# Moving row sums, projections and scaled results in a graph-attention and nucleus-diffusion kernel, and measuring the second pair's first points on VectorE

## The chip, the cores and the metric

The kernel runs on one core of a Trainium2 chip. The core has TensorE (PE, with its weight loads shown apart as PEld), VectorE (DVE), ScalarE (ACT), GpSimd (POOL) and SyncE (SP, which here only issues DMAs). Each engine works through its own queue in order; engines wait for each other by semaphores. The metric is the device time of one execution in microseconds, median over runs.

## What is computed

Two graph layers on N = 2708 nodes with 512 features, each with a layer norm and relu ahead of it and a residual around it. Layer 0 is graph attention with 8 heads of 64. Layer 1 runs two diffusion steps; each takes softmax rows of a learned similarity, keeps of every row the largest entries up to 0.9 of its mass, and mixes three products:

```
# layer 0
feats = einsum('nf,hfd->hnd', h, W)
attn  = softmax(leaky_relu(e_self + e_neigh) + mask)
x     = x + relu(einsum('hnm,hmd->hnd', attn, feats) + b)
# layer 1, steps s = 0, 1; S = adj + I
Rf = S / rowsum(S);  Rb = S / colsum(S)
A  = nucleus(softmax((Xa @ W1) @ W2 @ (Xa @ W3).T), 0.9)
Xf, Xb, Xa = Rf @ Xf, Rb @ Xb, A @ Xa
Z += Xf @ U1[s] + Xb @ U2[s] + Xa @ U3[s]
x  = x + layernorm(h + Z)
```

## The kernel before

Nodes are handled in NT = 22 tiles of 128 rows, the last with 20. "Step 1" below is the first diffusion step, s = 0 in the code; "step 2" is s = 1.

**Layer 0** works on chunks of six tiles of columns (`tchunks`: 6, 6, 6, 4), and in each chunk on two groups of four heads (`gi` = 0, 1). For each group a loop runs over all 22 row tiles `t`: VectorE makes four tiles `e` (L474), and TensorE multiplies them into PSUM banks `po` (L480). When a group is done ScalarE copies the banks out to `o_t` (L487), which frees them for the next group. At the start of a chunk the adjacency tiles are loaded (`a_f`, L449), cast on ScalarE (`a_c`, L451) and stored to `s_d` (L456). Then, for each of the chunk's tiles, `row_sums` (L337 to 349) loads the adjacency row in two halves into one buffer `arow` (SP, L345), adds each up on ScalarE (L346) and combines them on GpSimd.

What remains to be done to a tile of a finished chunk is cut into stages by `finished` (L359): `turned` transposes `o_t` into two PSUM banks (L372), `shared` divides by the sums (L388 to L397), `normed` and `cleared` make the next layer's input `v` (L416 is its relu on ScalarE), and `asked` transposes `v` (L423), copies it to `v_t` (L425), splits it into high and low parts and calls `project` (L171): eight matmul instructions (L176), two ScalarE copies (L181, L182), three GpSimd operations and a store of keys and queries. The dictionary `later` hangs these stages on steps `gi * NT + t` of the next chunk's loop (L483, L496): tile i of the old chunk has its stages at steps 3i to 3i + 3 and 3i + 5. The two banks (`pn0`, `pn1`) have one buffer each; `asked` transposes into the first and projects into the second. In the last chunk the stages run after the loop. In layer 0 the order on each engine is found by a planner, which takes what it considers ready and falls back on program order.

**Step 1 and step 2** have an order written by hand for TensorE, ScalarE, VectorE and SP (`manual_schedule`, L1293). They work on pairs of tiles (11 pairs), in a loop over g = -1 ... 10 (L1346). Pass g does the search of pair g + 1 and the attention of pair g:

- `Logits.products` (L558) multiplies queries with all keys (L567) and copies the results to `p` (L569). `p` has four buffers, so that those of pair g + 2 are those of pair g.
- `maxima` (L594, VectorE) take the row maximum; `exp` (L571) returns a list of steps: for each tile `root` and `full` (L601 with exp at half scale, L608), then `points` (GpSimd, L613 to L621), which guesses three thresholds. With `looks` there follow an empty step, twelve *looks* (ScalarE passes over `p`, L601 with `nth`: three thresholds, two functions, two tiles), and `masses` (GpSimd, L624 to L626), which makes of them the mass above each threshold.
- `search` (L734) finds the cut on VectorE. With an `Opened` handed to it, it starts from the masses of the looks (`ready`, L688; `bracket`). Without one it first measures them itself, six passes of L680 on VectorE, one for each threshold and tile. Then follow rounds of two L680, and `finish` (L874 to L809).
- In its second round `search` calls `early`, which appends the steps of the pair after next to the list `fills` and takes that pair's maxima. Before `finish` it calls `late`, in which the attention of pair g runs.
- `attended` (L1132) is a generator of twelve groups n = 0 ... 11: transpose a piece of `keep` (L1143), copy it to `at` (L1147), multiply with the values (L1165). From group `first` on it issues two steps of `fills` per group up to n = 8, then one; each group also takes one step of `others`, the products with the adjacency matrix (`part`, L1011).
- `mixed` (L1195) applies the third weight matrix (L1212), copies the results `yo` (L1219) and issues eight more fills. `late` then issues whatever fills are left.

`part` works through the adjacency products: 22 steps of loads and matmuls (L1042), then `across`, `through` (L1059) and `scaled` (L1069), which copies four results out of PSUM with a row factor and leaves their splitting (L197, L198) in the list `pending`. In pass g = -1 of step 1 there is no attention yet; `late` (L1395) issues there, in this order: four fills (root and full of both tiles of pair 1), the last `scaled`, eleven steps of the next `part`, and eleven more fills. The remaining four go into `looks` and are issued between the first groups of pair 0's attention (L1378). `pending` is emptied on VectorE after the first search (L1439).

Of the kernel before, what the change touches and what calls it, by code (L numbers as in the profile page):

```python
# [54 lines left out]
def kernel(  # L55
# [26 lines left out]
    NT = -(-N // P)  # L82
# [9 lines left out]
    G = 2  # L92
# [126 lines left out]
    with ExitStack() as l0:  # L219
# [139 lines left out]
        def finished(t, o_t, c0, bank, final):  # L359


            pr = rows[t]
            pns, held = [], []

            def turned():
                xt = work.tile([P, D], F32, name="xt0", bufs=4)
                nc.sync.dma_start(out=xt[:pr], in_=x[cols[t], :])
                held.append(xt)
                for g in range(NG):
                    pns.append(bank(g))  # L370
                    for k in range(len(beside)):
                        nc.tensor.transpose(pns[g][:pr, k * P:(k + 1) * P], o_t[:, g, k, c0:c0 + pr], ident)  # L372

            def shared():
                den = small.tile([P, H], F32, name="den")
                rden = small.tile([P, H], F32, name="rden")
                o = work.tile([P, D], F32, name="o", bufs=4)
                held.append(o)
                o3 = o.rearrange("p (h d) -> p h d", h=H)

                def halves(x, n):
                    return x[:, :2 * n].rearrange("p (i d) -> p i d", i=2)

                def turns(g):
                    return pns[g][:pr, :3 * P].rearrange("p (i d) -> p i d", i=2)

                for g in range(NG):
                    nc.vector.tensor_scalar(halves(den[:pr, g * HG:], 2), turns(g)[:, :, P::P // HG],  # L388
                                            lone_n[:pr, t:t + 1], None, op0=OP.add)
                nc.vector.reciprocal(rden[:pr], den[:pr])  # L390
                for g in range(NG):
                    c = slice(g * HG * DH, (g + 1) * HG * DH)
                    nc.vector.scalar_tensor_tensor(halves(o[:pr, c], 2 * DH), halves(fsum[:pr, c], 2 * DH),
                                                   lone[:pr, t:t + 1], turns(g)[:, :, :P], op0=OP.mult, op1=OP.add)
                eng = nc.vector if final else nc.gpsimd
                eng.tensor_mul(o3[:pr], o3[:pr], rden[:pr].unsqueeze(2).to_broadcast([pr, H, DH]))
                eng.tensor_add(o[:pr], o[:pr], b_b[:pr])  # L397

            def normed():
                xt, o = held  # L400
                nc.vector.scalar_tensor_tensor(o[:pr], o[:pr], 0.0, xt[:pr], op0=OP.max, op1=OP.add)
                held.extend(moments(small, o[:pr], pr))
                with_beta(o)

            def with_beta(o):
                xt = held[0]
                nc.gpsimd.tensor_add(xt[:pr], o[:pr], beta_b[:pr])
                nc.gpsimd.dma_start(out=xb_d[cols[t], :], in_=xt[:pr])

            def cleared():  # L410
                _, o, mean, rs = held
                v = turn.tile([P, D], F32, name="v")
                held.append(v)
                shift = small.tile([P, 1], F32, name="shift")
                nc.vector.scalar_tensor_tensor(shift[:pr], mean, -1.0, rs, op0=OP.mult, op1=OP.mult)
                nc.scalar.activation(v[:pr], o[:pr], AF.Relu, scale=rs, bias=shift[:pr])  # L416
                nc.gpsimd.dma_start(out=va_d[cols[t], :], in_=v[:pr])

            def asked():
                v = held[4]  # L420
                pt = bank(0).rearrange("p (k d) -> p k d", k=KD)
                for k in range(KD):
                    nc.tensor.transpose(pt[:, k, :pr], v[:pr, k * P:(k + 1) * P], ident[:pr, :pr])  # L423
                v_t = work.tile([P, KD, P], F32, name="v_t", bufs=2)
                nc.scalar.copy(v_t[:, :, :pr], pt[:, :, :pr])  # L425
                split_rows(halves, nc.gpsimd, v[:pr], t, vhl_d)
                project(halves, bank(1), v_t, t, 0, bufs=2)

            def rest():
                unasked.append((t, held[4]))  # L430

            return [turned, shared, normed, cleared, rest if final else asked]

        later = {}
        unasked = []
        for ci, tiles in enumerate(tchunks):
# [4 lines left out]
            for t in range(NT):  # L441
# [12 lines left out]
                    d = slice(t * P - n0, t * P - n0 + pr)  # L454
                    nc.gpsimd.tensor_tensor(a_f[:pr, d], a_f[:pr, d], ident[:pr, :pr], op=OP.add)
                nc.sync.dma_start(out=s_d[t * P:(t + 1) * P, n0:n0 + wide], in_=a_f[:, :wide])  # L456
            for t in tiles:
                row_sums(t)
            r_bs += [shares(grp, n0, cw) for grp in hgroups[1:]]
            o_t = work.tile([P, NG, len(beside), WC], F32, name="o_t", bufs=1)  # L460
            halfs = -(-cw // 512)
# [517 lines left out]
    for s in range(STEPS):  # L979
        last = s == STEPS - 1  # L980
        with ExitStack() as st:
# [136 lines left out]
            def paced(steps, n):  # L1118
                for step in steps[:n]:
                    step()  # L1120
                del steps[:n]
# [171 lines left out]
            with tc.manual_schedule(engines={PE, ACT, DVE, SP}):  # L1293
# [48 lines left out]
                    paced(loads, len(loads))  # L1342
                done = []
                ready = None
                looks, left = [], []
                for g in range(-1, NP):  # L1346

                    fills = []
# [25 lines left out]
                        fills += heads + [lambda: paced(counts, len(counts))]  # L1374
                    if g >= 0:
                        final = g == NP - 1 and not last
                        att = attended(pairs[g], *ready, fills, others, 1 if final else 3 if g else len(tgroups) + (1 if last else -1))
                    while looks:  # L1378
                        next(att)
                        paced(looks, 2)  # L1380

                    def early(g=g):
                        if g + 2 < NP:
                            fills.extend(lg[g + 2].exp())
                        first, *more = lg[g + 2].maxima if g + 2 < NP else [lambda: None]

                        def begin():
                            if g >= 0:
                                paced(pending, len(pending))
                            first()  # L1390

                        return (begin, lambda: [x() for x in more], lambda: [stats() for stats, _ in norms],
                                lambda: [rest() for _, rest in norms])

                    def late(g=g):  # L1395
# [24 lines left out]
                        if last:  # L1420
                            paced(fills, len(fills))
                        else:
                            paced(fills, 2 * G)
                            paced(others, 1)
                            others.extend(part(half, 2))
                            paced(others, NT // 2)
                            paced(fills, 2 + 3 * G * NA // 2)
                            looks.extend(fills)
                        if last:
                            paced(others, len(others))  # L1430

                    if g + 1 < NP:
                        opened = None
                        if g >= 0:
                            opened = Opened(lg[g + 1], True, junk)
                            opened.bracket()
                        ready = search(lg[g + 1], opened, junk, early, late)
# [44 lines left out]
```

## Time and profile before

Three runs took 3465.6, 3473.28 and 3474.12 us; the median is 3473.28. The profile comes from one execution more, which took 3485.01 us, with a span of 3483.2 us from the first to the last instruction. Busy time by stage, in us (a busy TensorE is not one at its peak):

| stage | from to | long | PE | DVE | ACT | POOL | granted clock |
|---|---|---|---|---|---|---|---|
| layer 0, features | 0 to 137 | 137 | 116.5 | 54.6 | 34.8 | 52.0 | 1.00 |
| layer 0, chunks | 137 to 945 | 808 | 734.6 | 716.1 | 186.3 | 295.6 | 0.94 |
| step 1 | 945 to 2185 | 1240 | 1163.7 | 684.4 | 678.8 | 285.0 | 0.98 |
| step 2 | 2185 to 3483 | 1298 | 1190.6 | 1127.6 | 601.5 | 291.0 | 0.97 |

A row of a timeline reads: start in us, length in us, engine, line of the kernel, operation, what it writes <- what it reads, shape, how many in a run, and in brackets how long the engine stood idle before and what released it. The granted clock is the share of full TensorE speed that the chip allowed in that stretch.

### The profile page before, as it was taken

To read this page: it belongs to the slowest core of one execution; us is meant where nothing else is said; L and a number is where in the kernel's file an instruction comes from. 1 tells how busy PE (TensorE), PEld (TensorE's weight loads), DVE (VectorE), ACT (ScalarE), POOL (GpSimd) and SP (SyncE) were. 2 spreads that over 40 slices of the span, in tenths; PEclk is the share of its full clock that TensorE was granted. 3 is DMA by queue.
4 is the path that set the end of the run, shared out by engine and by line. 5 is a ranking of instruction groups with operands and counts; after the bars stand their busy time and mean duration, and the time that the engine had idled before them with its cause. 6 is when DMAs were issued, how large, how long until landed. Compare 5 with 4: busy or idle time off the path is not lost. (4 is left out here: it accounts for less than half of the span.)

```text
span 3483.2 us, 44354 instructions
## 1 busy us (share of the span) xinstructions
PE 3205.4 (92%) x16033; PEld 1707.6 (49%) x16033; DVE 2582.7 (74%) x4485; ACT 1501.5 (43%) x2219; POOL 923.6 (27%) x1091
## 2 busy tenths in 40 slices
PE   8988899899988999999999999899989999988898
PEld 4542333333455446455464643555555555555554
DVE  4577899888947655463655643887999899988984
ACT  2333231011036675564667521265644554455610
POOL 4212743605231221221222222110230232213211
PEclk9998999999999999999999998999999999999999
DMA  4478554222286336244452634766444554556453
GB/s 134 157 235 267 193 169 144 75 94 80 76 299 235 113 106 208 99 166 165 142 198 98 212 112 134 263 237 203 146 156 157 202 177 144 190 175 225 150 209 123
DMA packets 240046, 580.65 MB, mean 167 GB/s; under 512 B 32863, under 2 KB 66107, under 8 KB 239657
## 3 DMA queue, kind: packets, MB, share of 16 engines
q1 hardware_dynamic: 217721, 503.38, 43.3%
q0 software_dynamic: 22064, 74.09, 5.6%
q8 instruction: 127, 2.08, 0.2%
q14 instruction: 134, 1.10, 0.1%
HBM read 471.68 MB, written 105.68 MB: 166 GB/s over the span
## 5 line engine op out<-in xcount | busy, mean ns | idle before, releaser
L1165 PE MATMUL a<-va,at 128*128 128x512 f32 (+2 forms) x1936 | 887.8, 598 | 4.9 <-ACT at L1147 4.9
L480 PE MATMUL po<-e,fw 128*32 128x384 f32 (+3 forms) x7392 | 685.1, 507 | 58.5 <-DVE e L474 29.4
L474 DVE SCALAR_TENSOR_TENSOR e<-r_b,kk,a_c 128x768 f32<-128x768 f32 (+3 forms) x704 | 667.3, 1007 | 76.9 <-PE po L480 67.9
L601 ACT ACTIVATE junk_a<-p,nth 128x2708 uint8<-128x2708 f32 (+1 forms) x240 | 612.8, 2553 | 35.3 <-POOL nth L616 30.8
L1039 PE MATMUL q<-hl,s_r 128*128 128x512 f32 x1936 | 545.4, 430 | 66.4 <-DMA s_r<-s_d 46.0
L1165 PEld LDWEIGHTS a<-va,at 128*128 128x128 f32 (+2 forms) x1936 | 338.2, 186 | 374.6 <-issue 342.8
L1039 PEld LDWEIGHTS q<-hl,s_r 128*128 128x128 f32 x1936 | 370.1, 195 | 229.4 <-issue 68.2
L480 PEld LDWEIGHTS po<-e,fw 128*32 128x32 f32 (+1 forms) x7392 | 256.0, 112 | 451.5 <-issue 270.2
L1147 ACT COPY at<-t 128x512 f32<-128x512 f32 (+3 forms) x308 | 140.8, 478 | 647.1 <-PE t L1143 643.3
L680 DVE SCALAR_TENSOR_TENSOR junk<-p,th 128x2708 bf16<-128x2708 f32 (+1 forms) x132 | 409.5, 3102 | 3.0
L1059 PE MATMUL q<-u_k,v 128*128 128x512 f32 x704 | 318.2, 594 | 1.1 <-ACT v L1049 1.1
L1042 PE MATMUL q<-s_r,hl 128*128 128x512 f32 (+1 forms) x1056 | 283.2, 414 | 28.8 <-DMA s_r<-s_d 17.9
L1042 PEld LDWEIGHTS q<-s_r,hl 128*128 128x128 f32 x1056 | 196.8, 192 | 108.5 <-issue 54.1
L1059 PEld LDWEIGHTS q<-u_k,v 128*128 128x128 f32 x704 | 134.0, 191 | 159.8 <-issue 155.0
L569 ACT COPY p<-t 128x452 f32<-128x452 f32 (+2 forms) x264 | 130.9, 537 | 172.5 <-PE t L567 131.9
L876 DVE MAX8 vn<-keep 128x8 f32<-128x2708 f32 (+1 forms) x66 | 196.8, 2981 | 2.3
L567 PE MATMUL t<-keys,q_t 128*128 128x452 f32 x528 | 156.4, 420 | 40.1 <-ACT p L569 39.5
L594 DVE TENSOR_REDUCE nmx<-p 128x1 f32<-128x2708 f32 (+1 forms) x44 | 130.5, 2967 | 65.4 <-ACT p L569 65.4
L1212 PE MATMUL a<-u_k,v_t 128*128 128x512 f32 (+1 forms) x352 | 169.0, 619 | 5.5 <-ACT yo L1219 3.3
L155 POOL TENSOR_SCALAR ln_rs<-ln_mv 128x1 f32<-128x1 f32 x66 | 49.7, 754 | 407.9 <-DVE ln_mv L154 406.7
L1143 PEld LDWEIGHTS t<-ident,keep 128*128 128x128 f32 (+1 forms) x968 | 114.7, 139 | 77.0 <-issue 47.3
L1143 PE MATMUL t<-ident,keep 128*128 128x128 f32 (+1 forms) x968 | 145.2, 272 | 3.1 <-ACT p L569 3.0
(311 smaller groups left out, 3436.2 us busy)
## 6 DMA issues: line engine op xcount, KB each, us to landing
hl<-vhl_d SPq DMA_DIRECT2D x132, 512.0 KB
s_r<-s_d SPq DMA_DIRECT2D x264, 256.0 KB
hl<-fhl_d SPq DMA_DIRECT2D x132, 512.0 KB
hl<-bhl_d SPq DMA_DIRECT2D x132, 512.0 KB
u_k<-in_L_gnn_U_dram SPq DMA_DIRECT2D x184, 256.0 KB
arow<-in_adj_dram SPq DMA_DIRECT2D x42, 677.0 KB
s_d<-a_f SPq DMA_DIRECT2D x66, 384.0 KB
s_r<-s_d SPq DMA_DIRECT2D x132, 192.0 KB
```

Source lines behind the costliest of these rows:

```text
L474: nc.vector.scalar_tensor_tensor(es[i][:pr, :cw], r_b[:pr, i, :cw], kk[:pr, t, grp[i]:grp[i] + 1], a_c[t][:pr, :cw], op0=OP.max, op1=OP.mult)
L480: nc.tensor.matmul(po[k][n][q * w:(q + 1) * w, :b - a], lhsT=of if d < DH else of.to_broadcast([pr, w]), rhs=es[i][:pr, a:b], start=(t == ...
L567: nc.tensor.matmul(pl[:, :c1 - c0], lhsT=q[:, i], rhs=self.keys[:, c0:c1], start=(i == 0), stop=(i == 1))
L601: nc.scalar.activation(junk[:pr], self.p[i][:pr], func, **kw)
L680: nc.vector.scalar_tensor_tensor(self.junk_b[:pr], p, th, p, op0=OP.is_ge, op1=OP.mult, accum_out=dst)
L876: v.max(vs, keep[0][:pr])
L1039: nc.tensor.matmul(half[j], lhsT=s_r[:, j * P:(j + 1) * P], rhs=hl[:, h], start=(c == 0 and h == 0), stop=(c == NT - 1 and h == 1))
L1042: nc.tensor.matmul(half[j][:, :w], lhsT=hl[:, h, j * P:(j + 1) * P], rhs=s_r[:, :w], start=(c == 0 and h == 0), stop=(c == NT - 1 and h == 1))
L1059: nc.tensor.matmul(half[j], lhsT=across_t[-1][k][:, j * P:(j + 1) * P], rhs=u_k, start=(start and k == 0), stop=(start and k == KD - 1))
L1143: nc.tensor.transpose(pt[:rows[c], j, :pr], keep[i][:pr, cols[c]], ident[:pr, :pr])
L1165: nc.tensor.matmul(pa[:pr], lhsT=at[:rows[c], j, :pr], rhs=va[:rows[c], c, :], start=(c == 0), stop=(c == NT - 1))
L1212: nc.tensor.matmul(pz[i][:rows[t]], lhsT=v_t[i][:, k, :rows[t]], rhs=u_k, start=(k == 0), stop=(k == KD - 1))
```

## The change

In layer 0, `asked` no longer calls `project`; a new stage `answered` does, which `later` places at step 3i + 6. `row_sums` of a chunk's tile i is no longer called ahead of the chunk's loops, but hung on step NT + 3i, in the loop of the second head group.

In step 1, pair 1 gets no looks (`exp(looks=last or g >= 0)`), and its search gets no `Opened`, so that VectorE measures its three thresholds. The list `looks` and its loop go; the fills in the attention of pair 0 begin with group 7 (`len(tgroups) + 1`) instead of group 5. In pass g = -1, the last `scaled` is issued after two fills instead of four, and `points` is the last fill. Step 2 keeps its order.

```diff
--- before.py
+++ after.py
@@ -423,13 +423,16 @@
                     nc.tensor.transpose(pt[:, k, :pr], v[:pr, k * P:(k + 1) * P], ident[:pr, :pr])
                 v_t = work.tile([P, KD, P], F32, name="v_t", bufs=2)
                 nc.scalar.copy(v_t[:, :, :pr], pt[:, :, :pr])
+                held.append(v_t)
                 split_rows(halves, nc.gpsimd, v[:pr], t, vhl_d)
-                project(halves, bank(1), v_t, t, 0, bufs=2)
+
+            def answered():
+                project(halves, bank(1), held[5], t, 0, bufs=2)
 
             def rest():
                 unasked.append((t, held[4]))
 
-            return [turned, shared, normed, cleared, rest if final else asked]
+            return [turned, shared, normed, cleared] + ([rest] if final else [asked, answered])
 
         later = {}
         unasked = []
@@ -454,8 +457,8 @@
                     d = slice(t * P - n0, t * P - n0 + pr)
                     nc.gpsimd.tensor_tensor(a_f[:pr, d], a_f[:pr, d], ident[:pr, :pr], op=OP.add)
                 nc.sync.dma_start(out=s_d[t * P:(t + 1) * P, n0:n0 + wide], in_=a_f[:, :wide])
-            for t in tiles:
-                row_sums(t)
+            for i, t in enumerate(tiles):
+                later.setdefault(NT + 3 * i, []).append(lambda t=t: row_sums(t))
             r_bs += [shares(grp, n0, cw) for grp in hgroups[1:]]
             o_t = work.tile([P, NG, len(beside), WC], F32, name="o_t", bufs=1)
             halfs = -(-cw // 512)
@@ -1342,7 +1345,7 @@
                     paced(loads, len(loads))
                 done = []
                 ready = None
-                looks, left = [], []
+                left = []
                 for g in range(-1, NP):
 
                     fills = []
@@ -1374,14 +1377,11 @@
                         fills += heads + [lambda: paced(counts, len(counts))]
                     if g >= 0:
                         final = g == NP - 1 and not last
-                        att = attended(pairs[g], *ready, fills, others, 1 if final else 3 if g else len(tgroups) + (1 if last else -1))
-                    while looks:
-                        next(att)
-                        paced(looks, 2)
+                        att = attended(pairs[g], *ready, fills, others, 1 if final else len(tgroups) + 1 if not g else 3)
 
                     def early(g=g):
                         if g + 2 < NP:
-                            fills.extend(lg[g + 2].exp())
+                            fills.extend(lg[g + 2].exp(looks=last or g >= 0))
                         first, *more = lg[g + 2].maxima if g + 2 < NP else [lambda: None]
 
                         def begin():
@@ -1420,18 +1420,18 @@
                         if last:
                             paced(fills, len(fills))
                         else:
-                            paced(fills, 2 * G)
+                            paced(fills, G)
                             paced(others, 1)
+                            paced(fills, G)
                             others.extend(part(half, 2))
                             paced(others, NT // 2)
-                            paced(fills, 2 + 3 * G * NA // 2)
-                            looks.extend(fills)
+                            paced(fills, len(fills))
                         if last:
                             paced(others, len(others))
 
                     if g + 1 < NP:
                         opened = None
-                        if g >= 0:
+                        if g >= (0 if last else 1):
                             opened = Opened(lg[g + 1], True, junk)
                             opened.bracket()
                         ready = search(lg[g + 1], opened, junk, early, late)
```

## The prediction

> **What bounds the kernel.** I read the windows by stage first, then the groups with their waits, then the timelines of single engines where TensorE stands idle. TensorE is busy 92% of 3483.2 us, so only its idle stretches can be won, or lengthened. The change touches two: the attention chunks of layer 0 (137 to 945 us, TensorE busy 734.6 of 808) and the opening of step 1 (945 to about 1205 us).
>
> Layer 0 alternates between TensorE and VectorE, which hand each other the `e` tiles. It stops dead twice, near 230 and 330 us. The 5 us windows around the first (PE, PEld, DVE, ACT, POOL busy, then granted clock, DMA share, GB/s):
>
> ```profile
> 225.00:230.00 5.00, 1.90 (x24) 0.50 (x16) 3.81 (x4) 1.43 (x2) 0.00 (x0) 0.82 0.38 109
> 230.00:235.00 5.00, 0.00 (x0) 0.00 (x0) 0.00 (x0) 1.42 (x2) 0.62 (x3) 0.50 0.40 132
> 235.00:240.00 5.00, 0.00 (x0) 0.00 (x0) 0.00 (x0) 1.73 (x4) 0.00 (x0) 0.50 0.84 316
> ```
>
> ScalarE's timeline says why: it stands in its queue at row sums whose loads are late, and the PSUM evacuations (L487) that TensorE needs come behind them.
>
> ```profile
> 232.33 1.33 ACT L346 ACTIVATE arow<-arow 128x1354 f32<-128x1354 f32 x1 [4.04 <-DMA arow<-in_adj_dram]
> 238.27 1.33 ACT L346 ACTIVATE arow<-arow 128x1354 f32<-128x1354 f32 x1 [4.52 <-DMA arow<-in_adj_dram]
> 239.60 1.98 ACT L487 COPY o_t<-po 128x384 f32<-128x384 f32 x5
> ```
>
> The second idle kind recurs once per tile in chunks 1 and 2: the projection (L176) waits for `v_t`, whose copy stands on ScalarE behind the next tile's L416. TensorE, ScalarE and VectorE timelines of one tile:
>
> ```profile
> 624.89 2.08 PE L176 MATMUL pn<-v_t,kw 128*128 128x128 f32 x8 [3.03 <-ACT v_t L425]
> ...
> 623.55 0.81 ACT L416 ACTIVATE v<-o,shift,ln_rs 128x512 f32<-128x512 f32 x1 [17.78 <-DVE shift L415]
> 624.27 0.56 ACT L425 COPY v_t<-pn 128x512 f32<-128x512 f32 x1
> ...
> 629.75 2.25 DVE L474 SCALAR_TENSOR_TENSOR e<-r_b,kk,a_c 128x768 f32<-128x768 f32 x2 [3.12 <-PE po L480]
> ```
>
> In the opening of step 1 TensorE waits for the scaled results to leave PSUM, then, at the end of pair 0, for ScalarE to be through with its looks:
>
> ```profile
> 1068.33 3.91 PE L1042 MATMUL q<-s_r,hl 128*128 128x512 f32 x10 [8.59 <-ACT yo L1069]
> ...
> 1067.61 2.40 ACT L1069 ACTIVATE yo<-q,cinv 128x512 f32<-128x512 f32 x4
> ...
> 1194.88 0.98 ACT L569 COPY p<-t 128x452 f32<-128x452 f32 x2
> ...
> 1195.48 1.12 PE L567 MATMUL t<-keys,q_t 128*128 128x452 f32 x4 [2.36 <-ACT p L569]
> ```
>
> **Row sums: counted at 0.** Layer 0 has no hand-written order; the planner places instructions by readiness, with program order as the tie-break. The loads show how far it pulls work without predecessors forward:
>
> ```profile
> L345 SPq DMA_DIRECT2D arow<-in_adj_dram x44: 302/328/807, 182.5 to 474.7; - x44
> ```
>
> Chunks 2 and 3 only begin near 572 and 780 us, yet all their row sums are loaded by 475. Moving `row_sums` down half a chunk (some 90 us) leaves it just as ready, on engines just as free (SP and ScalarE have nothing else between 200 and 240). Of all pairs that run together, the move reverses only a row sum of chunk 0 against chunk 0's first L487. So I expect the same nine ahead of L487, one load per 5.7 us, and the same stalls. Bounds: the two boundaries cost VectorE 16.0 and 18.2 us, so at best about -30 us; an unlucky new order costs up to +10.
>
> **Projection one step later: -13 us.** Nothing is added; eight L176 instructions per tile move behind the rest of the next step (38 more L480 instructions, 3.4 to 5.4 us in the timeline). `v_t` was 3.0 us late in the six worst cases, so it is there in time. TensorE waited 6.4 us at L176 in chunk 1 and 12.1 in chunk 2; VectorE idled in consequence 6.35 us (3.11, 0.52, 1.92, 0.80) and 9.9 us (3.12, 0.82, 0.90, 2.51, 2.54). What comes next is VectorE, busy otherwise, so the ceiling is its 16.2 us; chunk 3 is VectorE-bound already and gives nothing. What the move adds: the transposes of the tile after next (L372) take the bank that the projection has just filled, and so wait for L181 and L182. In chunk 2 these start 0.03 us after a typical projection and end 0.5 us later, covered by the transposes into the other bank. In chunk 1 the remaining row sums stand on ScalarE; there I keep 4 of 6.35, and 9 of 9.9 in chunk 2.
>
> A rule to weigh: the Trainium skill ("TensorE: Matmul & The Clock Gate", What's actually happening) says that the array falls to half clock only after an idle window of about 3.4 us. By it, a 3.0 us wait costs 3.0 us. The rows disagree: after it the eight projections took 2.08 us at 624.89 and 2.07 at 665.03, against 1.16 elsewhere. By the rows the six long waits are worth some 4 us more on TensorE; VectorE's ceiling takes that away again, so -13 stands either way.
>
> **Scaled results between the two root/full pairs: -8.2 us at first.** ScalarE ends the first tile's full at 57.8 (times of this part are us after 1000) and waits till 62.1 for the second maximum. The four L1069 (2.4 us) fit in there; the last product ends at 59.7, so L1042 starts there instead of at 68.33. The 11 steps after it are paced by loads that are issued as slots come free, so the whole block, 99.5 at its end, moves to about 91. The next thing due is the end of the search of pair 0 (VectorE, 91.8), which frees `p` for the L569 copies: these start at 91.9 instead of 100.08. Attention of pair 0 shifts by -8.2.
>
> **No looks for pair 1: +15.5 us.** ScalarE loses 12 looks (2.55 + 0.19 each). VectorE gains six masses; the same six for pair 0 took 1016.87 to 1035.45, 18.6 us. They stand behind the eight split pieces that end at 114.8 and wait for stores (6.91, 3.70, 1.97 us) while TensorE's loads hold the DMA queues. With the loads over by then I take 109 (the four pieces at 1237 waited only 3.19 us). Then:
>
> ```profile
> 1118.57 0.17 DVE L688 TENSOR_TENSOR pts<-top,pts 128x6 f32<-128x6 f32 x1 [3.73 <-POOL pts L626]
> ...
> 1132.29 2.97 DVE L594 TENSOR_REDUCE nmx<-p 128x1 f32<-128x2708 f32 x1
> ...
> 1142.20 2.97 DVE L594 TENSOR_REDUCE nmx<-p 128x1 f32<-128x2708 f32 x1
> ```
>
> L688 moves from 118.6 to 127.7, the maxima of pair 2 (L594) end at 144.4 and 154.3. The start of the fills moves from group 5 to 7, where the copy of `at` 8 now falls at 139.5. Root and full wait there for the first maximum (done 149.9; stall about 0.3), then for the second (done 159.8); `at` 10 comes at 160.4 where TensorE wants it at 156.6: 3.8. With the look behind it, the second `v_t` of the pair is copied by 170.2 instead of 173.8, so 3.6 of the 8.2 us remain. If the split pieces don't end sooner, 5 us more go; if they end at 106, about 3 fewer.
>
> Then the tail. Group 5 to 7 is four fills fewer in attention. In the old run five looks run there, four and three inside `mixed`, none after. In the new one it is one, four and four, with three left, which `late` issues ahead of the next pair's L569. ScalarE reaches L569 at 170.2 + 10.5 + 1.7 + 10.7 + 1.0 + 8.0 = 202.2, against 194.9: +7.3. TensorE, which waited 2.36 there, now waits about 13. The search of pair 2 begins with the same delay, so nothing later catches up: pairs 1 to 10 are TensorE-bound and merely shift.
>
> Another rule speaks against this edit: "SBUF — State Buffer" (SBUF: two separate sides) says ScalarE has ports of its own, while a VectorE operation with two SBUF inputs shuts out a GpSimd operation that reads SBUF for its whole length. The row: L618 took 4.21 us beside the masses of pair 0, 1.35 without. By the rule the 18.6 us would cost GpSimd one mass, 3 us; by the timeline it then has only stores to issue, and I count 0.
>
> **The sum.** -13 + 7.3 = -5.7 us on the profiled 3485.0 (span 3483.2 and 1.8 around it), or 3479.3. The median shown is 11.7 below the profiled time; the same difference from it gives 3468.
>
> **Rivals.** *Row sums really leave the first halves*: they spread over the second halves, L487 finds ScalarE free, both stops go (-30): about 3438. For it speaks only the wording of the edit; against it, loads at 475 us. *A new wait on the projection's bank* (slower): in chunk 1, L372 follows L176 at once, L181 and L182 stand behind a row sum whose load takes some 4.5 us, four tiles in turn: +18, chunk 1's gain lost, so -9 + 18 + 7.3 = +16, 3490. It decides from 2.7 us per tile. For it: ScalarE waits 165.8 us for these loads in all; against: old L181s there waited at most 1.3 us. *The planner puts the projections where they were*, so layer 0 gives nothing: +7, 3481.
>
> **Chances.** Forecast 0.55 (own range 3458 to 3482: layer 0 from -18 to -4, step 1 from +3 to +13), row sums 0.14, bank 0.16, no effect in layer 0 0.15. Outside 3440 to 3489 lie half of the row-sum and half of the bank case. Faster by over 0.3% (about what a measurement can tell from no change): 0.14 + 0.13 = 0.27; slower: 0.16, half of the last case: 0.24; between: 0.49.
>
> **What would show it.** Right: L346 before 240 us as now, no 3 us waits at L176, L1042 near 1060, six L680 behind the split pieces, about 13 us before L567 near 1202. Wrong: L346 only in second halves; L372 waiting for L182; no gap before L567, which would make step 1 a gain.

## The result and the profile after

The changed kernel takes 3478.42 us (median of 20 runs, 3463.52 to 3510.39), the kernel before 3473.51 us beside it. The ratio is 1.0008 with a 95% interval of 0.9991 to 1.0024: no difference that can be measured. 3468 had been forecast, with a range of 3458 to 3482, and "within 0.3%" held the largest chance. The range and the class came true; the small gain of 5.7 us does not show (by the ratio +2.8 us, -3 to +8).

Below the surface much moved. The profiled execution took 3465.86 us, some 13 below the median of its kernel, where the profile of before is some 11 above its own. So sums are read stage by stage here, over the profiles of all runs, and not from one pair. From the end of `asked` on, line numbers are 3 higher than before (L480 is now L483, L567 is L570, L1165 is L1168).

**Layer 0, the first stop.** Windows of 5 us around it, columns as in the prediction:

```profile
227.00:232.00 5.00, 0.00 (x0) 0.00 (x0) 1.54 (x2) 1.42 (x2) 0.62 (x3) 0.50 0.37 110
232.00:237.00 5.00, 0.65 (x6) 0.21 (x10) 0.00 (x0) 2.50 (x6) 0.00 (x0) 0.50 0.93 359
```

ScalarE's timeline there:

```profile
234.50 1.33 ACT L346 ACTIVATE arow<-arow 128x1354 f32<-128x1354 f32 x1 [4.39 <-DMA arow<-in_adj_dram]
...
235.84 1.98 ACT L490 COPY o_t<-po 128x384 f32<-128x384 f32 x5
```

and the loads of the tile `arow` (operation and count, then shortest, median and longest issue in ns, then first and last start):

```profile
L345 SPq DMA_DIRECT2D arow<-in_adj_dram x44: 301/328/1067, 180.7 to 469.6; - x44
```

A row sum still stands ahead of the copies of `o_t`, and the 44 loads still begin at 181 us and are through at 470. The edit moved nothing.

**Layer 0, the projection.** TensorE's timeline in chunks 1 and 2:

```profile
440.88 0.55 PE L372 MATMUL pn<-ident,o_t 128*128 128x128 f32 x3 [3.25 <-ACT kq_b L182]
...
614.25 1.16 PE L176 MATMUL pn<-v_t,kw 128*128 128x128 f32 x8 [0.46 <-ACT v_t L425]
```

The 3 us waits ahead of L176 are gone: 0.5 us is left of 18.5 in the whole layer. The feared new wait, L372 behind L182, is there once, for 3.3 us. Another new wait is not on TensorE at all: VectorE now waits for GpSimd (see e1_projection). Layer 0 ends (last L483) at 919.2 us, not at 943.5.

**Step 1.** TensorE first, then ScalarE and VectorE:

```profile
1032.14 2.41 PE L1045 MATMUL q<-s_r,hl 128*128 128x512 f32 x8
...
1066.59 7.51 PE L570 MATMUL t<-keys,q_t 128*128 128x452 f32 x20 [6.25 <-ACT p L572]
...
1135.86 6.62 PE L1168 MATMUL a<-va,at 128*128 128x512 f32 x8 [3.61 <-ACT at L1150]
...
1180.38 7.97 PE L570 MATMUL t<-keys,q_t 128*128 128x452 f32 x20 [11.63 <-ACT p L572]
```

```profile
1066.00 0.97 ACT L572 COPY p<-t 128x452 f32<-128x452 f32 x2 [24.82 <-DVEq L961]
...
1119.86 0.20 ACT L607 ACTIVATE nmx<-nmx 128x1 f32<-128x1 f32 x1 [5.10 <-DVE nmx L597]
...
1129.78 0.20 ACT L607 ACTIVATE nmx<-nmx 128x1 f32<-128x1 f32 x1 [3.34 <-DVE nmx L597]
...
1179.81 0.95 ACT L572 COPY p<-t 128x452 f32<-128x452 f32 x2
```

```profile
1084.50 3.03 DVE L683 SCALAR_TENSOR_TENSOR junk<-p,th_a 128x2708 bf16<-128x2708 f32 x1
...
1116.86 2.97 DVE L597 TENSOR_REDUCE nmx<-p 128x1 f32<-128x2708 f32 x1
```

L1045 no longer waits for the scaled results (8.59 us before), and the copies to `p` start in the very moment in which the search of pair 0 ends (1066.00). That is the gain. Then the six passes of VectorE begin at 1084.5, behind the split pieces, and push the maxima of pair 2 back; ScalarE waits for both, TensorE once for ScalarE (3.61 us), and at the end three looks are left over, behind which TensorE waits 11.63 us, against 2.36 before.

Lengths that can be told apart over all profiles (worked out from the starts and ends of the named instructions):

| stretch | kernels without the edit | kernels with it |
|---|---|---|
| layer 0, start to TensorE's restart after its second stop near 340 | 340.0 to 343.6, mean 341.5 (5 profiles) | 337.5 to 346.6, mean 341.5 (5, later projection) |
| from there to the first L388 of chunk 1's tiles | 230.1 to 231.9, mean 231.0 | 225.5 to 226.9, mean 226.2 |
| from there to the first L388 of chunk 2's tiles | 223.5 to 226.9, mean 226.1 | 213.1 to 213.5, mean 213.3 |
| from there to the last `po` matmul | 141.8 to 142.0 | 141.5 to 141.7 |
| step 1: end of pair 0's search (start of L969) to the L569 ahead of pair 1's attention | 100.3 to 103.1, mean 101.2 (8) | scaled results alone (e3, e5): 102.3, 101.3; no looks alone (e4): 118.7; both: 113.8, 113.8 |
| step 1, whole: to the first matmul of step 2 | 1232.4 to 1242.4, mean 1237.4 (8) | scaled results alone: 1230.6, 1239.4; no looks alone: 1257.4; both: 1246.8, 1249.7 |

So by the traces layer 0 gives 4.8 + 12.8 + 0.3 = 17.9 us. The opening of step 1 loses 113.8 - 101.2 = 12.6; over the whole of step 1 it is 1248.2 - 1237.4 = 10.8, where the kernels without the edit alone differ by 10.

### The profile page after: what moved, and what is told of

Its sections match the earlier page's. It is cut to its first block, busy times and chain, and to the rows that moved or that the text cites. A ratio compares the mean times of both kernels' runs of the same rounds, so it can differ in the third digit from the quotient of the medians.

```text
span 3464.1 us, 44348 instructions
## 1 busy us (share of the span) xinstructions
PE 3187.4 (92%) x16033; PEld 1698.3 (49%) x16033; DVE 2588.8 (75%) x4497; ACT 1471.4 (42%) x2195; POOL 928.7 (27%) x1088
## 3 DMA queue, kind: packets, MB, share of 16 engines
q8 instruction: 127, 2.08, 0.3%
## 5 line engine op out<-in xcount | busy, mean ns | idle before, releaser
L1168 PE MATMUL a<-va,at 128*128 128x512 f32 (+2 forms) x1936 | 890.5, 600 | 7.6 <-ACT at L1150 7.5
L483 PE MATMUL po<-e,fw 128*32 128x384 f32 (+3 forms) x7392 | 677.0, 503 | 61.6 <-DVE e L477 37.4
L477 DVE SCALAR_TENSOR_TENSOR e<-r_b,kk,a_c 128x768 f32<-128x768 f32 (+3 forms) x704 | 659.5, 996 | 46.7 <-PE po L483 38.1
L604 ACT ACTIVATE junk_a<-p,nth 128x2708 uint8<-128x2708 f32 (+1 forms) x228 | 582.1, 2553 | 36.4 <-POOL nth L619 32.1
L1042 PE MATMUL q<-hl,s_r 128*128 128x512 f32 x1936 | 536.3, 424 | 61.8 <-DMA s_r<-s_d 45.3
L1168 PEld LDWEIGHTS a<-va,at 128*128 128x128 f32 (+2 forms) x1936 | 339.5, 187 | 379.2 <-issue 343.7
L483 PEld LDWEIGHTS po<-e,fw 128*32 128x32 f32 (+1 forms) x7392 | 257.3, 112 | 446.3 <-issue 262.6
L1042 PEld LDWEIGHTS q<-hl,s_r 128*128 128x128 f32 x1936 | 363.1, 192 | 224.3 <-issue 68.8
L1045 PE MATMUL q<-s_r,hl 128*128 128x512 f32 (+1 forms) x1056 | 279.9, 409 | 16.7 <-DMA s_r<-s_d 15.1
L1045 PEld LDWEIGHTS q<-s_r,hl 128*128 128x128 f32 x1056 | 193.2, 189 | 95.7 <-issue 53.4
L572 ACT COPY p<-t 128x452 f32<-128x452 f32 (+2 forms) x264 | 132.4, 536 | 197.1 <-PE t L570 116.5
L570 PE MATMUL t<-keys,q_t 128*128 128x452 f32 x528 | 162.5, 433 | 58.0 <-ACT p L572 57.4
```

The source lines that it names most:

```text
L477: nc.vector.scalar_tensor_tensor(es[i][:pr, :cw], r_b[:pr, i, :cw], kk[:pr, t, grp[i]:grp[i] + 1], a_c[t][:pr, :cw], op0=OP.max, op1=OP.mult)
L483: nc.tensor.matmul(po[k][n][q * w:(q + 1) * w, :b - a], lhsT=of if d < DH else of.to_broadcast([pr, w]), rhs=es[i][:pr, a:b], start=(t == ...
L570: nc.tensor.matmul(pl[:, :c1 - c0], lhsT=q[:, i], rhs=self.keys[:, c0:c1], start=(i == 0), stop=(i == 1))
L604: nc.scalar.activation(junk[:pr], self.p[i][:pr], func, **kw)
L1042: nc.tensor.matmul(half[j], lhsT=s_r[:, j * P:(j + 1) * P], rhs=hl[:, h], start=(c == 0 and h == 0), stop=(c == NT - 1 and h == 1))
L1045: nc.tensor.matmul(half[j][:, :w], lhsT=hl[:, h, j * P:(j + 1) * P], rhs=s_r[:, :w], start=(c == 0 and h == 0), stop=(c == NT - 1 and h == 1))
```

## The experiments

| label | what runs | median, us (runs) | before beside it, us | ratio, 95% interval |
|---|---|---|---|---|
| e0_before_again | before, a second profile | 3472.01 (1) | 3474.98 | |
| e1_projection | later projection alone | 3462.95 (22) | 3474.98 | 0.9972, 0.9959 to 0.9984 |
| e2_row_sums | row sums' edit alone | 3476.57 (20) | 3478.69 | 0.9992, 0.9980 to 1.0004 |
| e3_scaled | scaled results alone | 3477.59 (14) | 3474.98 | 1.0010, 0.9994 to 1.0026 |
| e4_no_looks | no looks alone | 3491.63 (12) | 3474.98 | 1.0046, 1.0031 to 1.0061 |
| e5_proj_scaled | projection and scaled results | 3467.44 (22) | 3478.09 | 0.9968, 0.9956 to 0.9981 |
| e7_first5 | changed kernel, fills from group 5 | 3467.39 (6) | 3478.69 | 0.9973, 0.9942 to 1.0004 |
| e8_after_again | changed kernel again | 3478.18 (14) | 3478.09 | 1.0002, 0.9982 to 1.0022 |
| e12_held_alone | row sums held back by `e` | 3521.79 (4) | 3478.69 | 1.0114, 1.0097 to 1.0131 |
| e9_held | the same, later projection | 3515.74 (4) | 3478.69 | 1.0086, 1.0063 to 1.0109 |
| e13_second_half | row sums held back by `o_t` | 3460.22 (21) | 3473.69 | 0.9959, 0.9948 to 0.9970 |
| e14_second_half_proj | the same, later projection | 3448.26 (6) | 3473.69 | 0.9931, 0.9909 to 0.9953 |

### The parts one at a time

**e0_before_again** has no edit.

> The kernel before once more, to see what one execution differs from another by. Layer 0's last L480 came at 943.0 us in its first profile and at 918.7 in that of the changed kernel; step 1, from there to the first matmul of step 2, took 1242.9 us against 1247.3. Theory (these are properties of the kernels): 943 within 4 us and 1243 within 3. Rival (the spread of 10 us and more between runs of one kernel lies in layer 0's loads): layer 0 ends elsewhere, by 8 us or more, and the 24 us between the two profiles are partly luck.

It took 3472.01 us; layer 0 ended at 937.2 and step 1 took 1239.9 us, against 943.5 and 1242.4 in the first profile. Layer 0 is 6.3 us off, beyond the 4 us of the theory and short of the 8 of the rival. This is the scatter against which the rest is read.

**e1_projection**

```diff
+                held.append(v_t)
...
-                project(halves, bank(1), v_t, t, 0, bufs=2)
+            def answered():
+                project(halves, bank(1), held[5], t, 0, bufs=2)
...
-            return [turned, shared, normed, cleared, rest if final else asked]
+            return [turned, shared, normed, cleared] + ([rest] if final else [asked, answered])
```

> The projection's step alone moves. Theory: no wait of 3 us at L176 is left, layer 0 ends 10 to 17 us earlier than in the kernel before, step 1 is as long as before; ratio 0.995 to 0.998. Rival (layer 0's gain comes from the row sums): L176's waits go, but layer 0 ends within 4 us of before, since VectorE or the wait of L372 for L182 takes the place; ratio 0.999 to 1.001.

By the medians it is worth 3475 x 0.0028 = 9.7 us (5.6 to 14.2). In the trace layer 0 ends at 920.2; L372 waits once, 4.0 us, for L182. So the gain is real, and the rival with the bank is an event of a single tile. What VectorE waited for in chunk 2 (us in total, times, longest), in the kernel before:

```profile
DVE e L474 <- PE po L480: 20.4, 12, 4.2
```

and in this one:

```profile
DVE o L401 <- POOL o L397: 9.3, 4, 2.4
DVE e L477 <- PE po L483: 3.0, 3, 2.5
```

The wait for TensorE falls by 17.4 us, and a wait for GpSimd that was not there before takes 9.3 of them. It stands behind L397: when a tile's L396 and L397 fall due, GpSimd is still at the projection of an earlier tile (L186 to L189), and from L390 to the end of L397 it takes 5.0 and 5.7 us in two tiles, against 3.9 before. In chunk 1 the same two waits go from 12.2 to 4.1 and from 2.6 to 11.3 us, which cancel out.

**e2_row_sums**

```diff
-            for t in tiles:
-                row_sums(t)
+            for i, t in enumerate(tiles):
+                later.setdefault(NT + 3 * i, []).append(lambda t=t: row_sums(t))
```

> Only the edit that moves the row sums. Theory: the planner undoes it, the program is the old one with other buffer numbers, so the ratio is 1.000 within its interval, the row-sum loads still run from about 182 to 475 us, and TensorE stops near 230 and 330 us as before. Rival (row sums leave the first halves): about 30 us less, ratio 0.991.

In its trace every engine runs the same instructions in the same order as in e0_before_again. Its loads of row sums run from 183.4 to 472.2 us, TensorE stops for 12.3 and 14.1 us, and the ratio is 0.9992. The planner undoes the edit, as forecast.

**e3_scaled**

```diff
-                            paced(fills, 2 * G)
+                            paced(fills, G)
                             paced(others, 1)
+                            paced(fills, G)
```

> Only the last scaled results move between the two root/full pairs; the looks stay. Theory: L1042 starts right after L1059 instead of 8.6 us later, L567 of pair 2 then waits a little for the end of the search (under 2 us), and 7 to 8 us stay to the end, since the looks end earlier too: ratio 0.997 to 0.999. Rival (nine looks between L1042 and L567 hold ScalarE): L567's copies stand behind the looks, which do not start earlier than before, so that under 2 us remain; ratio 0.9995 to 1.0005.

Nothing was gained that the medians show; it is the rival's case. TensorE's and ScalarE's timelines of this kernel:

```profile
1053.15 2.39 PE L1042 MATMUL q<-s_r,hl 128*128 128x512 f32 x8
...
1090.15 7.52 PE L567 MATMUL t<-keys,q_t 128*128 128x452 f32 x20 [9.30 <-ACT p L569]
```

```profile
1089.49 0.19 ACT L601 ACTIVATION_READ_ACCUMULATOR junk_a<-p,nth 128x1 f32 x1
1089.59 0.95 ACT L569 COPY p<-t 128x452 f32<-128x452 f32 x2
```

The wait ahead of L1042 is gone, and 37 us later the same length of wait stands ahead of L567. The search of pair 0 is over at 1083.1, but ScalarE works until 1089.5 through nine looks of pair 1 that stand in its queue ahead of L569. With the looks kept, ScalarE and VectorE set the time at which `p` is free, not TensorE, so giving TensorE its products sooner buys nothing that can be measured: the search ends 57.2 us after the start of L1059, in the eight profiles with the old step 1 after 56.7 to 61.7. e5_proj_scaled shows the same wait again, 11.59 us. Step 1 as a whole took only 1230.6 us here, but 1239.4 in e5_proj_scaled with the same step 1: that is scatter.

**e4_no_looks** is the changed step 1 (fills from group 7 included) with the scaled results in their old place:

```diff
-                            fills.extend(lg[g + 2].exp())
+                            fills.extend(lg[g + 2].exp(looks=last or g >= 0))
-                        if g >= 0:
+                        if g >= (0 if last else 1):
                             opened = Opened(lg[g + 1], True, junk)
...
```

> Only the looks of pair 1 go (with the fills from group 7); scaled stays after all four fills. Theory: six L680 stand behind the split pieces, the maxima of pair 2 come 9 to 15 us later, three looks are left after mixed, and attention of pair 1 starts 12 to 20 us later than in the kernel before, against the end of the first search; ratio 1.003 to 1.006. Rival (the wait at L567 in the changed kernel comes of the earlier start that scaled gives, so that without it all falls into place): pair 1 starts at most 5 us later; ratio under 1.0015.

+0.46% is +16.0 us (10.8 to 21.2). TensorE's timeline has the two waits that make most of it:

```profile
1160.53 1.11 PE L1143 MATMUL t<-ident,keep 128*128 128x128 f32 x4 [4.02 <-ACT v_t L165]
...
1212.00 5.02 PE L567 MATMUL t<-keys,q_t 128*128 128x452 f32 x12 [12.82 <-ACT p L569]
```

`v_t` stands on ScalarE behind the root that waits for the late maximum; the three left-over looks stand ahead of L569.

### Where the price of the looks' removal lies

**e7_first5** starts the fills two groups sooner again:

```diff
-    ... 1 if final else len(tgroups) + 1 if not g else 3)
+    ... 1 if final else len(tgroups) - 1 if not g else 3)
```

> The changed kernel with one difference: the steps of pair 1 start at group 5 of pair 0's attention, not at group 7. Theory: no looks are left over at the end, so the 11.6 us wait ahead of pair 1's L570 falls to about 2.5 us; but the first root now stands on ScalarE some 11 us longer for the maximum that VectorE takes behind its six passes, with the copies of at behind it, and TensorE waits there some 8 to 12 us: 3475 to 3482 us, no gain over the changed kernel. Rival (the left-over looks are the loss, and the late maxima cost nothing): 9 us less than the changed kernel, about 3469.

```profile
1128.15 0.20 ACT L607 ACTIVATE nmx<-nmx 128x1 f32<-128x1 f32 x1 [13.88 <-DVE nmx L597]
...
1134.87 6.02 PE L1168 MATMUL a<-va,at 128*128 128x512 f32 x8 [11.15 <-ACT at L1150]
...
1186.81 1.11 PE L570 MATMUL t<-keys,q_t 128*128 128x452 f32 x4 [0.81 <-ACT p L572]
```

The wait changes its place, from L570 to L1168, and keeps its size (11.63 to 11.15 us). The first line is ScalarE, which waits 13.88 us for the late maximum ahead of the copies of `at`. Step 1 takes 1246.9 us, as in the changed kernel (1246.8, 1249.7). From the end of pair 0's search to the next L572 it is 111.5 us, so that only 2.3 of the 12.6 us come back. By this trace the late maxima are the cause, and where TensorE pays for them, in the middle of the attention or at its end, is a choice. The times do not bear that out: the median of 3467.39 lies below the 3475 to 3482 of the theory and at the 3469 of the rival. With six runs the interval reaches from 0.9942 to 1.0004 and overlaps that of the changed kernel, so they do not refute it either.

**e5_proj_scaled** is the change without the looks' removal and without the row sums' edit, which changes no order.

> The later projection and the scaled results, with the looks of pair 1 kept: the change without its last edit (and without the row sums' edit, which changes no order). Theory: step 1 is 5 to 8 us shorter than before, as in the trace of the scaled results alone, and layer 0 ends 15 to 22 us sooner; the medians have shown half of that for the projection and nothing for the scaled results, so 3458 to 3466 us, ratio 0.995 to 0.9985, and the changed kernel's loss against this one, 12 to 20 us, is the price of the looks' removal. Rival (scaled results and projection disturb each other): ratio 1.000.

Ratio 0.9968. Against it the changed kernel (1.0002 in the same comparison, 1.0008 in the first) is 0.34 to 0.40% slower: beside the other edits the removal of the looks costs 12 to 14 us by the medians. The 16 us that it costs alone are not clear of that by the medians. The traces do show a difference, from the end of pair 0's search to the L569 ahead of pair 1's attention: 118.7 - 101.2 = 17.5 us alone, 113.8 - 101.8 = 12.0 on top of the scaled results. So the scaled results come to something once the looks are gone: ScalarE is then idle when the search ends, and L572 starts at once (1066.00 above), where in e4_no_looks, with the scaled results in their old place, L569 starts 5.1 us after it.

**e8_after_again** is the changed kernel.

> The changed kernel once more, for a second profile and a second interval. Theory: layer 0 ends near 920 us, step 1 takes 1244 to 1250 us (before: 1232 to 1242 in the profiles with its step 1), the six passes of VectorE stand ahead of pair 1's rounds, TensorE waits some 11 us ahead of pair 1's L570, and the ratio is 1.000 within 0.002. Rival (the step 1 of the first profile was a slow one): step 1 near 1237 us.

Layer 0 ended at 920.6, step 1 took 1249.7, TensorE again waited 3.61 us at L1168 and 11.64 at L570. The first profile was not an odd one.

### Moving the row sums for real

The forecast held the two stops near 230 and 330 us to be the row sums' doing, and the edit to be without effect. If both are right, a move that the planner can't undo gains. Two ways to hold the loads back were tried.

**e12_held_alone** makes each load wait for the `e` tile of its step:

```diff
                 arow = adjp.tile([P, w], F32, name="arow", bufs=1)
+                nc.gpsimd.tensor_copy(arow[:1, :1], after[0][:1, :1])
...
+                    after[:] = es[:1]
                     for stage in later.pop(gi * NT + t, ()):
```

> The kernel before with the row sums moved for real: ahead of each load of a row sum, GpSimd writes one element of its buffer from the e tile of the step at which the edit hangs it, so that the load can't start before that step; nothing else is changed. If the row sums' loads are what stops TensorE near 230 and 330 us: ScalarE is free when L490 falls due, both stops go, about 25 to 35 us less, ratio about 0.991. If the stops have another cause, or the row sums only stand in the way of other work in the second halves: ratio 0.998 to 1.003.

It is 40 us slower, outside both expectations. VectorE's waits in layer 0 (us in total, times, longest) say why:

```profile
DVE e L476 <- POOL arow L343: 72.5, 19, 6.0
DVE e L476 <- PE po L482: 31.3, 23, 3.1
```

The second row was 67.9 us in the kernel before: the stops did go. But GpSimd's own waits (109.7 us of them for the row sum's L347) show that its one-element copy waits until the row sum before it has left `arow`, and meanwhile keeps an `e` buffer which VectorE needs. The hold put a longer wait in the place of the one removed.

**e9_held** has the later projection besides.

> The same real move of the row sums together with the later projection, step 1 as in the kernel before. Theory: the two gains lie at different places and add up, 30 + 10 = 40 us, ratio about 0.9885. Rival (the projection's gain came from waits that the row sums cause, so the two are one gain): as the real move alone.

Same fault, same result: 30 us slower instead of 40 faster (layer 0 ends at 977.6).

**e13_second_half** takes another hold, once per chunk and from a tile that nobody is short of:

```diff
+                if t % 6 == 0 and i == 0:
+                    nc.gpsimd.tensor_copy(arow[:1, :1], o_t[:1, 0, len(beside) - 1, :1])
...
             o_t = work.tile([P, NG, len(beside), WC], F32, name="o_t", bufs=1)
+            for i, t in enumerate(tiles):
+                later.setdefault(NT + 3 * i, []).append(lambda t=t, o_t=o_t: row_sums(t, o_t))
```

> The kernel before with the row sums in the second half of each chunk, held by a wait that costs nothing elsewhere: once per chunk GpSimd writes one element of arow from o_t, which is written when the first half's banks leave PSUM, so the chunk's first row sum can't start before that; no e tile is held any longer. Theory: the slowdown with the earlier hold came from the e tiles that GpSimd kept (VectorE waited 67 us for it); without it both long stops of TensorE for o_t (13 to 18 us each) are gone and nothing takes their place: 20 to 35 us less, ratio 0.990 to 0.994. Rival (the loads and casts of the next chunk, which share ScalarE and the DMA queues with the row sums there, are pushed late and stop VectorE at the next chunk's start): ratio 0.999 to 1.005.

ScalarE's timeline around 230 us:

```profile
225.34 1.07 ACT L489 COPY o_t<-po 128x384 f32<-128x384 f32 x2 [28.27 <-PE po L482]
...
236.10 1.34 ACT L348 ACTIVATE arow<-arow 128x1354 f32<-128x1354 f32 x1 [6.53 <-DMA arow<-in_adj_dram]
```

and TensorE's at the second stop:

```profile
317.66 6.29 PE L482 MATMUL po<-e,fw 128*32 128x384 f32 x48 [3.81 <-ACT o_t L489]
```

Now ScalarE waits for TensorE ahead of the copies, not TensorE for ScalarE. Of the two stops 3.8 us are left. The first `den` of chunk 0's tiles comes at 324.6 us, not at 351.0; chunk 3, which now carries row sums of its own, takes 146.9 us instead of 141.9. Layer 0 ends at 920.2, some 20 us sooner. The time falls by 0.41% (14 us; 10 to 18), less than the theory's 20 to 35 but clearly: the two stops are the row sums' doing.

**e14_second_half_proj** adds the later projection.

> The same with the projection one step later besides. Theory: the projection's gain of about 10 us lies in the first halves of chunks 1 and 2, the row sums' at the ends of chunk 0's two halves; they add up: 30 to 45 us less than before, ratio 0.987 to 0.991. Rival (part of the projection's gain came from the row sums that stood ahead of the copies in chunk 1): 3 to 6 us below the real move alone.

0.9931, and 0.9959 x 0.9972 is 0.9931: the gains add up, though the 24 us of both together stay below the 30 to 45 of the theory, as the row sums alone did. Layer 0 ends at 899.8 us. Windows of this kernel at the first stop (PE, PEld, DVE, ACT, POOL, clock, DMA share, GB/s):

```profile
220.00:225.00 5.00, 5.00 (x64) 1.99 (x58) 4.18 (x5) 1.44 (x3) 0.00 (x0) 1.00 0.41 116
225.00:230.00 5.00, 5.00 (x48) 1.71 (x44) 3.81 (x4) 2.19 (x5) 0.75 (x1) 0.71 0.85 303
230.00:235.00 5.00, 5.00 (x64) 1.92 (x60) 4.23 (x5) 2.25 (x4) 0.00 (x0) 0.95 0.43 135
```

TensorE runs through. This version, with step 1 as it was, beats both kernels, by some 24 us.

## Why the prediction was right, and where its terms were off

**Row sums, 0.** Right, and shown: the same instructions in the same order in the trace of e2_row_sums. The bound of -30 for a real move was wide: e13 gained 20 us in the trace and 14 by the medians. The tiles of chunk 0 come 24 us sooner (324.6 against 348.8 on average), and chunk 3 gives back 5 for its own row sums.

**Projection, -13.** The sign is right, the size too small in the trace (17.9 us; 4.8 in chunk 1, where 4 had been kept, and 12.8 in chunk 2, where 9 had been), and that it came so near is in part luck. The term "the ceiling is its 16.2 us" took VectorE's idle time, and it alone, for the gain. The wait for TensorE fell by more than was counted (8.1 and 17.4 us against 6.35 and 9.9), and the wait for GpSimd, which the forecast does not have, took 8.7 and 9.3 back. In chunk 1 VectorE's idle time is therefore almost what it was (20.6 and 19.9 us); in chunk 2 it fell from 25.3 to 16.6. The rest came from its busy time, which fell by 4.2 us in chunk 1 and by 4.8 in chunk 2: there 160 passes of `e` took 1130 ns each before and 1105 after. A pass with no GpSimd operation beside it takes 1.01 us in both kernels; those with more than 0.4 us of one beside them took 1.37 us before and 1.27 after (chunk 2, worked out from the records' starts and ends). So the difference lies in these, and moving GpSimd's work changed them; which operation does it was not tried.

**The new wait on the bank.** A rival with the right mechanism: L372 behind L182 happened in each of the five profiles with the later projection and the old row sums, in one tile or two (3.2 to 5.1 us in all), not in four tiles in a row.

**Scaled results, -8.2.** The step that failed is "the next thing due is the end of the search of pair 0 ... these start at 91.9 instead of 100.08". Taken alone, as the sum took it, this is not so: e3 shows nine looks ahead of L569 and a 9.3 us wait there. It holds only once the looks are gone, and the text counted it ahead of that edit. The two edits aren't independent; the net of both was what the forecast needed, and there the order of counting doesn't matter. The size was taken from one profile, and a high one: the first copy started 8.3 us behind the end of the search there, and 5.6 to 6.6 us behind it in the other seven profiles with the old step 1.

**No looks, +15.5.** This was counted on top of the scaled results, so it has to be compared with the 12 to 14 us of the medians and the 12.0 of the traces; the +16.0 measured alone is that of another step 1. Its chain can be laid beside the trace, in us after the end of pair 0's search: the maxima end at 53.8 and 63.7 (forecast 52.6 and 62.5), TensorE's stalls are 0.48 and 3.61 (0.3 and 3.8), the second `v_t` is copied by 82.3 (78.4), ScalarE reaches L572 at 113.8 (110.4), TensorE waits 11.6 there (13). What was left out is that the eight L1168 after the 3.61 us stall took 6.62 us instead of 3.60: 3.0 of the 3.4 us by which the tail came later (the granted clock is 0.51 from 1134.9 to 1141.8). The prediction had weighed just that clock rule in layer 0 and then not used it here.

**The net.** Step 1: +7.3 forecast, +12.6 in the traces up to the L569 ahead of pair 1's attention. The 5.3 us between them are the 3.4 of the tail and some 2 of the high 8.3. Layer 0: -13 forecast, -17.9 in the traces. That the two errors offset each other is luck. The forecast of -5.7 us agrees with the traces; of the two measured intervals the first (-3 to +8) leaves it out and the second (-6 to +8) just holds it.

**What stays open.** The traces make the change -5 to -7 us; the medians make it +0.7 (interval -6 to +8) and +2.8 (-3 to +8). For the projection alone it is -17.9 against -9.7 (5.6 to 14.2), for the real move of the row sums -20 against -14. The gain in chunks 1 and 2 is several times the scatter between profiles (the table above), so it is clear; step 1 varies by 10 and step 2, untouched, by 13 (1292.1 to 1305.6), and no profile shows that these grow when layer 0 shrinks. Each profile is of one execution, and five of the seven with a shorter layer 0 are of one below the median of their kernel, by up to 13 us. Why the medians credit only part of the gain was not found.

## What to carry to other kernels

- Under a planner that orders by readiness, moving a call in the source may move nothing, as here. A dependence did move it, and what it hangs on matters: holding every load on `e` cost 40 us, holding the first load of each chunk on `o_t` gained 14. (The two differ in the tile and in the number of holds; the trace puts the loss down to the `e` buffers.)
- A wait that is removed can reappear at the next instruction that the same engine stands behind, or on an engine that was not looked at. Nine looks ahead of one copy ate the whole gain of the scaled results, and GpSimd's queue took half of what the later projection spared VectorE.
- Work taken from one engine's queue and given to another's is paid where the receiver's next result is due. ScalarE and TensorE did not wait for the six passes of 3 us on VectorE but for the two maxima behind them, and the removal cost 12 to 18 us.

## What the runs showed of the hardware

- **The half clock followed waits of 3.0 us, and not only waits.** The Trainium skill ("TensorE: Matmul & The Clock Gate", What's actually happening) gives an idle window of about 3.4 us; by it none of the waits named here would have mattered. In the kernel before, six waits of 3.02 to 3.03 us stand ahead of L176. Around the end of five of them (from 1.9 us before it to 1.4 us after it) the granted clock fell to 0.50, for 3.4 or 6.8 us; only some of the eight matmuls fell into these stretches, which is why they took 2.07, 1.16, 2.08, 1.16, 2.07 and 1.55 us. After the second of these waits the clock fell only once the eight were done (0.50 from 422.7 to 426.1). Two waits of 1.8 and 1.1 us with 0.84 us of work between them had the same effect in e1_projection (0.51 from 630.4 to 633.8, after 3.4 us in which TensorE was busy for 1.13). And in e14_second_half_proj it came with no wait at all, behind 48 matmuls of the last row tile, which has 20 rows (0.50 from 227.1 to 230.5). Whether the 20 rows are the reason was not tried.
- **The scatter between runs goes with the granted clock.** In 35 runs of the kernel before, the six at a mean clock of 0.967 took 3485.0 us on average, the nine at 0.970 took 3473.9; in 41 runs beside e1_projection it was 3477.0 and 3470.3. Which of the two, a longer wait or a lower clock, comes first is not shown.
